# A four-layer graph attention kernel on one core: how the first layer's table is made, and when its first gathers are prepared

## The chip, the core and the metric

The kernel runs on one core of a Trainium2 chip. A core has engines that each work through their own queue of instructions in order: TensorE (PE; its weight loads are listed apart as PEld), VectorE (DVE), ScalarE (ACT), GpSimd (POOL) and SyncE (SP, which here issues most transfers). They meet through semaphores, and share an on-chip memory (SBUF), the matmuls' accumulators (PSUM) and 16 DMA engines.

The metric is device time in microseconds (us) of one execution. Before the change it is 3165.0 us, the median of 9 runs (3157.26 to 3171.3).

## The reference

Four different graph networks are stacked. Each is wrapped in a residual and a layer norm; all use one adjacency matrix `adj` of 4096 x 4096, whose density falls with the index of the row and of the column (0.4% in the mean). There are 256 channels.

```python
def _L0_gnn_ref(x, positions, curv_feats, adj, W, a_l, a_r, Wc, gate):
    N, IN_C, OUT_C, H, CF = (4096, 256, 256, 8, 6)
    h = (x @ W.T).reshape(n, H, D)                      # D = 32
    e_l = jnp.einsum('nhd,hd->nh', h, a_l)
    e_r = jnp.einsum('nhd,hd->nh', h, a_r)
    logits = jax.nn.leaky_relu(e_l[:, None, :] + e_r[None, :, :], negative_slope=0.2)
    curv_pair = jnp.abs(curv_feats[:, None, :] - curv_feats[None, :, :])
    curv_bias = jnp.einsum('ijf,hf->ijh', curv_pair, Wc)
    logits = logits + gate * curv_bias
    logits = jnp.where(mask, logits, jnp.float32(-1000000000.0))
    attn = jax.nn.softmax(logits, axis=1)
    out = jnp.einsum('ijh,jhd->ihd', attn, h)
    return out.reshape(n, H * D)
...
    # --- layer 0 (adj_resnorm) ---
    x = _layernorm(x + _L0_gnn_ref(x, ..., adj, ...), axis=-1)
    # --- layer 1 (adj_resnorm) ---
    x = _layernorm(x + _L1_gnn_ref(x, adj, ...), axis=-1)
    # --- layer 2 (adj_resnorm) ---
    x = _layernorm(x + _L2_gnn_ref(x, adj, ...), axis=-1)
    # --- layer 3 (adj_resnorm) ---
    x = _layernorm(x + _L3_gnn_ref(x, adj, ...), axis=-1)
    return x
```

Layer 1 is attention with one head, layer 2 with four, layer 3 is three attention layers in a row. The change lies in layer 0.

## The kernel before

**Edges in place of a matrix.** Layer 0 uses the sparsity. Rows (the nodes that receive) are cut into 32 row tiles of 128. Row tile 0, the densest, is done as dense matrix work by the generator `rows0` (L448 on; `cj` at L459 are its constants, `g` at L469 its loads, which it shares with later layers through a mask made of `at` tiles). Row tiles 1 to 31 are done edge by edge in `rows_by_edges` (L600 on).

**The projection and the table.** `layer0` (L767 on) first projects the 32 tiles of nodes (the loop over T, after L1139; four tiles share a load `xT`). The result goes to `V0`, 32 tiles of 128 x 278 f32: 8 heads of 33 values (VW = 264), 8 score factors and 6 curvature features. When all tiles are there, the maxima of the scores are taken (`extremes`, whose first step is L1162; `shifts`, `row_factors`), ACT makes exponentials (L1172, L1173), and in one loop over T DVE multiplies each tile by its factors (L1175) and SP writes it to `table0` in DRAM (L1177): 32 transfers of 139 KB, 4.55 MB together. `V0` lies in a pool (`l0_pro`) that ends with the projection.

**The lists.** Which edges a row has is found by class `Lists` (L848 on): a quarter of a row tile of `adj` is loaded (`ai`), ACT turns it to bf16 (L873, L874), DVE searches each piece for its ones (`max_index`, L905), sorts the finds (`max` L920, `match_replace` L922), and small steps end in `from_middle` (L942), which says where each row's edges stand in the row tile's edge list. One list is some 14 to 18 steps of a generator, `edge_lists`. Six steps are taken after every fourth projected tile; the others, while gathers run, by `lane` (14/EDGE_TILES steps per edge tile, so about one list per row tile, which keeps the lead that the projection gave). `prepared(c)`, called when a block asks for its list, takes the steps that are still lacking at once.

**Blocks.** A row tile's edges lie in 9 to 39 edge tiles of 128, cut into 64 blocks of 5 to 9 edge tiles. The steps of a block, in class `Block`:

- `middle`: calls `prepared`, then `u` on ACT (L630), from the constant `number` and `from_middle`
- `spread`: `of_row` on DVE (L635), products to `x` on PE (L639)
- `nodes` (L642 to L654): from `x` and the constants `place` and `count` to the index of every edge, `idx`, on DVE
- `gather` (L659): per edge tile one indirect DMA by POOL, which fetches 128 rows of `table0`; 445 in all. The buffer `g` comes from the pool `l0_got`, which holds three
- `differences`, `pair_terms`, `weights`: the curvature term, with the two tiles `dT` (L619, L620), and the edge's weight
- `values`: `g` times weight on DVE (L689)
- `rows`: `to_row` on ACT (L696, L697)
- `add`: per edge tile a matmul on PE (L702) into the row tile's accumulator `acc`; the last reader of `g`

The loop over the blocks (L735 on) interleaves the steps of blocks i to i+4: `spread` of i+3, then `values` of i, `gather` of i+2, `nodes` of i+3, `add` of i, `middle` of i+4, with `lane` between them. `lane` also issues jobs for later layers, among them single cells of `adj` by indirect DMA on POOL (L1020). `Ends0` finishes row tiles (L320 to L439).

**The order of instructions.** The program's order is not what each engine gets: a scheduler sets the order of the instructions of each engine when the kernel is built, and a new buffer waits for what last used its memory. A pool that is opened where another one ended waits for that pool as a whole.

**The start of `rows_by_edges`.** The constants `number`, `place`, `count` and the two `dT` are made there, after the table's loop: an iota on POOL, casts and memsets on DVE (L614 to L620, L706 to L712). Then the first blocks are prepared:

```python
            for i in range(3):
                at(i, "middle", "spread", "nodes")
                if i < 2:
                    at(i, "gather")
            at(3, "middle")
            at(0, "differences", "pair_terms", "rows", "weights")
```

Of the kernel before, what the change touches and what calls it, by code (L numbers as in the profile page):

```python
# [49 lines left out]
F32 = mybir.dt.float32  # L50
# [3 lines left out]
U16 = mybir.dt.uint16  # L54
I32 = mybir.dt.int32
# [25 lines left out]
def gnn_stack(ctx: ExitStack, tc: tile.TileContext, a: dict, out: bass.AP):  # L81
# [363 lines left out]
                for c, y in zip(cs, ys):  # L445
                    yield from self.proj.steps(c, y)

    def rows0(chunks, ends, ps, ps_s, ps_acc):  # L448

        with ExitStack() as st:
            two = st.enter_context(tc.tile_pool(name="l0_all_two", bufs=2))
            three = st.enter_context(tc.tile_pool(name="l0_all_three", bufs=2))
            got = st.enter_context(tc.tile_pool(name="l0_all_got", bufs=3 * JR))
# [141 lines left out]
            while due:  # L597
                add(*due.pop(0))

    def rows_by_edges(prepared, pair_w, ends, ps, lane, first):  # L600

# [4 lines left out]

        with ExitStack() as st:
            two = st.enter_context(tc.tile_pool(name="l0_two", bufs=2))  # L610
            got = st.enter_context(tc.tile_pool(name="l0_got", bufs=3))
            ps_acc = st.enter_context(tc.tile_pool(name="l0_acc", bufs=2, space=PSUM))
            ps_x = st.enter_context(tc.tile_pool(name="l0_x", bufs=2, space=PSUM))
            number = two.tile([P, BT, P], U16, name="number", bufs=1)  # L614
            place = two.tile([P, max(EDGE_TILES)], F32, name="place", bufs=1)
            count = two.tile([P, P], F32, name="count", bufs=1)
            dTs = [two.tile([ROW1 + 1, P], F32, name=f"dT{k}", bufs=1) for k in range(2)]
            for d in dTs:
                nc.vector.memset(d[0:ROW1], 0.0)  # L619
                nc.vector.memset(d[ROW1:], 1.0)  # L620

            class Block:
                def __init__(self, c, b, t0, n):
# [77 lines left out]
                    for t in range(n):  # L701
                        nc.tensor.matmul(acc, self.to_row[:, t], self.g[:, t, 0:VW], start=self.t0 + t == 0, stop=last and t == n - 1)  # L702

            number_i = two.tile([P, BT * P], I32, name="number_i", tag="to_row")  # L706
            nc.gpsimd.iota(number_i, pattern=[[1, BT * P]], base=0, channel_multiplier=0)
            nc.vector.tensor_copy(number.rearrange("p t r -> p (t r)"), number_i)
            nc.vector.tensor_copy(count, number_i[:, 1:P + 1])
            place_i = two.tile([P, max(EDGE_TILES)], I32, name="place_i", bufs=1)  # L710
            nc.gpsimd.iota(place_i, pattern=[[P, max(EDGE_TILES)]], base=1, channel_multiplier=1)
            nc.vector.tensor_copy(place, place_i)  # L712
# [12 lines left out]
            dense = first(lambda shape, name: ps_x.tile(shape, F32, name=name, tag="x"),  # L725
                          lambda shape, name: ps_acc.tile(shape, F32, name=name, tag="acc0", bufs=1))
            given = 0
            for i in range(3):
                at(i, "middle", "spread", "nodes")
                if i < 2:  # L730
                    at(i, "gather")
            at(3, "middle")
            at(0, "differences", "pair_terms", "rows", "weights")
            late = []
            for i, blk in enumerate(plan):  # L735
                c, n = blk.c, blk.n
                share = n // 4
                ends.put.extend(late)
                late = []
                at(i + 3, "spread")  # L740
                lane(share, c)
                at(i + 1, "differences")
                blk.values()
                at(i + 2, "gather")
                at(i + 1, "pair_terms")
                lane(share, c)
                at(i + 3, "nodes")
                lane(share, c)
                if blk.t0 == 0:
                    ends.until(c - 2)  # L750
# [19 lines left out]
    def layer0(proj):  # L770
        lin = 1.0 - 0.2
        with ExitStack() as st:
# [55 lines left out]
            ones8 = lp.tile([P, 8], BF16, name="ones8")  # L828
            nc.vector.memset(ones8, 1.0)
            near_by = [lp.tile([P, N + 8 * max(sum(k) for k in kinds)], BF16, name="near"), None]  # L830

            adj_pool = st.enter_context(tc.tile_pool(name="l0_adj", bufs=1))
            lists = st.enter_context(tc.tile_pool(name="l0_list", bufs=2))
# [285 lines left out]
            with ExitStack() as pr:  # L1119
# [19 lines left out]
                for T in range(NT):  # L1139
                    if T % ITS == 0:  # L1140
                        xT = xp.tile([P, 2, IC], F32, name="xT")
                        nc.sync.dma_start(xT, a["xT"][:, T * P:T * P + IC].rearrange("(k p) n -> p k n", p=P))
                        nc.vector.tensor_reduce(p0.xs[:, :, T:T + 1], xT, AX.X, ALU.add)
                    drain(p0.product(T, xT[:, :, T % ITS * P:(T % ITS + 1) * P]))
                    if T == ITS - 1:
                        pair_constants(pp, ps_p)
                        nc.vector.memset(by_head[:, :, :, D0:], 1.0)
                        nc.scalar.copy(V[:, :, VW + H0:], curv)
                        none = pp.tile([1, TW], F32, name="none")
                        nc.vector.memset(none, 0.0)  # L1150
                        nc.sync.dma_start(table0[N:N + 1, :], none)
                        drain(proj.prepare(ps))
                    if T % 4 == 3:
                        for _ in range(6):
                            next(edge_lists)
                p0.sums()
                nc.vector.tensor_copy(cs0, p0.cs)
# [2 lines left out]
                with tc.tile_pool(name="l0_st", bufs=1) as sp:  # L1160
                    g = sp.tile([P, NT, H0], F32, name="g0")
                    nc.vector.tensor_sub(g, f2, cw)  # L1162
                    hl, top = extremes(sp, ps_p, f2, H0, more=g)
                    neg_M, v_shift, sc = shifts(sp, top[:, 0, :], top[:, 1, :], lin, "l0")
                    row_factors(sp, ps_p, p0.f1, neg_M, top[:, 1, :], sc, lin, r0_d, side[:, :, 1:1 + H0])
                    nc.vector.tensor_copy(side[:, :, 0:1], neg_row.unsqueeze(1).to_broadcast([P, NC, 1]))
                    nc.vector.tensor_copy(side[:, :, 1 + H0:], curv)
                    nc.vector.tensor_sub(v_shift, v_shift, neg_M)
                    nc.vector.tensor_sub(v_shift, v_shift, top[:, 2, :])
                    v = sp.tile([P, NT, H0], F32, name="v0")  # L1170
                    for h in range(H0):
                        nc.scalar.activation(v[:, :, h], g[:, :, h], AF.Exp, bias=v_shift[:, h:h + 1])  # L1172
                        nc.scalar.activation(V[:, :, VW + h], f2[:, :, h], AF.Exp, bias=sc[:, h:h + 1], scale=-lin)  # L1173
                    for T in range(NT):
                        nc.vector.tensor_tensor(by_head[:, T], by_head[:, T],  # L1175
                                                v[:, T, :].unsqueeze(2).to_broadcast([P, H0, D0 + 1]), ALU.mult)
                        nc.sync.dma_start(table0[T * P:(T + 1) * P, :], V[:, T, :])  # L1177

            at_pool = st.enter_context(tc.tile_pool(name="l0_at", bufs=3))

# [37 lines left out]
            def lane_e(n, c):  # L1218

                for _ in range(n):  # L1220
                    lane(1, (14 / EDGE_TILES[c], 5 / EDGE_TILES[c]))
                    ends.step()

            rows_by_edges(prepared, pair_w, ends, ps, lane_e,
                          lambda ps_s, ps_acc: rows0(FIRST, ends, ps, ps_s, ps_acc))
            proj.sums()
            for k in range(2):
                drain(lanes[k][0])
# [445 lines left out]
    with tc.If(nc.values_load(over[0:1, 0:1], min_val=0, max_val=1) > 0):  # L1674
        with ExitStack() as st:
            pool = st.enter_context(tc.tile_pool(name="all_at", bufs=5))
            for ic in range(-(-DENSE[1] * PW // IC), NIC):
                for load in mask_bytes(pool, ic):
                    load()()
            p1 = first_projection()  # L1680
            ps = tags(st.enter_context(tc.tile_pool(name="all_ps", bufs=1, space=PSUM)), ["pa", "pb"])
            p1.load(st)
            drain(p1.prepare(ps))
            pool = st.enter_context(tc.tile_pool(name="all_acc", bufs=2, space=PSUM))
            ends = Ends0(p1, ps)
            for _ in rows0(NC, ends, ps, lambda shape, name: pool.tile(shape, F32, name=name, tag="s"),
                           lambda shape, name: pool.tile(shape, F32, name=name, tag="acc0")):
                ends.step()
            drain(ends.steps)
            p1.sums()  # L1690
# [54 lines left out]
```

## Time and profile before

| | |
|---|---|
| median of 9 runs | 3165.0 us (3157.26 to 3171.3) |
| the profiled execution: its own time | 3161.5 us |
| its span on the core | 3159.8 us |
| busy PE / PEld | 2574.6 us (81%) / 1800.5 us (57%) |
| busy DVE / ACT / POOL | 2277.9 (72%) / 1329.0 (42%) / 1976.2 us (63%) |
| gathers of layer 0 (L659) | 445, 517.1 us busy, mean 1162 ns |
| cells for later layers (L1020) | 251, 280.2 us busy, mean 1116 ns |
| chain that ended last | PE 51%: L1605 21%, L1515 12%, L1519 8% |

The whole span, split at four points of layer 0 (from the trace; the columns are the stretch, its length, and busy time with count for PE, PEld, DVE, ACT and POOL, then PE's granted clock, the share of time that the DMA engines were busy, and GB/s):

```profile
0.00:105.00 105.00, 58.02 (x328) 47.49 (x328) 78.64 (x403) 40.50 (x129) 6.96 (x107) 0.79 0.53 160
105.00:135.00 30.00, 4.21 (x49) 3.19 (x48) 25.56 (x98) 6.53 (x20) 1.37 (x2) 0.50 0.84 221
135.00:1150.00 1015.00, 636.99 (x5024) 489.21 (x5023) 817.99 (x3088) 585.42 (x1573) 758.20 (x656) 0.74 0.66 198
1150.00:1206.00 56.00, 28.65 (x101) 20.09 (x101) 25.93 (x95) 17.56 (x54) 24.47 (x28) 0.70 0.52 152
1206.00:3160.00 1954.00, 1846.71 (x10568) 1240.55 (x10568) 1329.79 (x3864) 679.00 (x2125) 1185.23 (x1083) 0.97 0.47 134
```

Read it by stage: up to 105 us the projection and the first lists, to 135 the table, to 1150 the gathers, to 1206 the last row tiles, and then layers 1 to 3. The share of busy time of an engine over the whole span is a mean over these stages; only within a stage does it say what limits it. Idle time of an engine is listed with its releaser, the event that came last before the engine went on.

### The profile page before, as it was taken

The page shows a single profiled execution, that of the slowest core. Times are in us where ns is not written, and L with a number is a line of the kernel's source. Part 1 is how long each engine was busy: PE and PEld are TensorE (multiplying, and loading weights), DVE is VectorE, ACT ScalarE, POOL GpSimd, SP SyncE. Part 2 cuts the span into 40 slices and gives each one's busy share as a digit, 9 for nine tenths or more (in the row PEclk, how much of TensorE's full clock was granted, in tenths as well). Part 3 has the DMA queues.
Part 4 walks back from the last instruction along what each step waited for, and adds up shares of the span by engine and source line. Part 5 has one row for each costly group of instructions (what it writes and reads, how often), then busy time and mean ns, then how long its engine had stood idle before and what let it go on. Part 6 is the DMA issues. An engine that isn't in the chain of part 4 may idle for free.

```text
span 3159.8 us, 53737 instructions
## 1 busy us (share of the span) xinstructions
PE 2574.6 (81%) x16067; PEld 1800.5 (57%) x16067; DVE 2277.9 (72%) x7545; ACT 1329.0 (42%) x3895; POOL 1976.2 (63%) x1874
## 2 busy tenths in 40 slices
PE   6266676656666556998999999998899999998997
PEld 5154454444445446996233333333788878887875
DVE  6777877888988856776878788886565556555666
ACT  3365565646666434776212222333222322232334
POOL 0267667777777856772475566651477647755775
PEclk8588776777876677998999999999999999999999
DMA  6567786657676447775333333331554454446654
GB/s 182 163 200 217 234 245 195 208 171 220 198 218 203 115 128 231 200 206 156 105 89 102 95 104 100 100 86 50 172 136 135 114 175 135 135 112 180 166 166 129
DMA packets 345937, 495.65 MB, mean 157 GB/s; under 512 B 120476, under 2 KB 252418, under 8 KB 345634
## 3 DMA queue, kind: packets, MB, share of 16 engines
q0 software_dynamic: 87600, 252.16, 28.6%
q1 hardware_dynamic: 239608, 223.19, 23.5%
q10 hardware_dynamic: 18432, 16.79, 1.6%
q8 instruction: 132, 2.16, 0.3%
q14 instruction: 165, 1.35, 0.1%
HBM read 426.20 MB, written 65.72 MB: 156 GB/s over the span
## 4 chain that ended last, share of the span: by engine, by line
PE 51%; DMA 3%; DVE 2%; ACT 2%; issue 1%; POOL 0%; SPq 0%; ACTq 0%; DVEq 0%; POOLq 0%
PE acc L1605 21%; PE num L1515 12%; PE den L1519 8%; PE ph L209 4%; PE acc L1414 4%; DMA g<-table,pair_idx 3%; PE xT_p L198 1%; PE pr L213 1%; DVE w L1599 1%; PE pt L1537 0%; ACT V L1585 0%; POOL g L1312 0%; DVE y L1617 0%; DVE y L314 0%; DVE bn_st L305 0%
## 5 line engine op out<-in xcount | busy, mean ns | idle before, releaser
L1312 POOL DMA_INDIRECT g<-table,pair_idx x1010 | 1120.4, 1109 | 514.8 <-PE den L1519 103.0
L659 POOL DMA_INDIRECT g<-table,idx x445 | 517.1, 1162 | 195.2 <-issue 119.2
L1605 PE MATMUL acc<-g,w 128*128 128x257 f32 x2448 | 574.1, 382 | 16.6 <-DVE w L1599 15.8
L1605 PEld LDWEIGHTS acc<-g,w 128*128 128x128 f32 x2448 | 458.3, 190 | 93.3 <-DVE w L1599 29.2
L1506 DVE SCALAR_TENSOR_TENSOR w<-R,g,mask 128x256 f32<-128x256 f32 x1004 | 438.9, 488 | 47.8 <-PE den L1519 47.4
L1599 DVE SCALAR_TENSOR_TENSOR w<-R,g,mask 128x256 f32<-128x256 f32 x612 | 292.4, 482 | 238.8 <-PE acc L1605 183.2
L1515 PE MATMUL num<-w,g 128*64 128x256 f32 x2008 | 367.6, 395 | 0.0
L1020 POOL DMA_INDIRECT pair_m<-in_adjT,cell x251 | 280.2, 1116 | 108.0 <-issue 46.6
L702 PE MATMUL acc<-g,to_row 128*128 128x264 f32 x890 | 301.3, 498 | 40.0 <-DVE g L689 31.3
L1605 PE MATMUL acc<-V,w 128*128 128x257 f32 x1152 | 285.2, 388 | 16.9 <-ACT V L1585 9.6
L702 PEld LDWEIGHTS acc<-g,to_row 128*128 128x128 f32 x890 | 214.0, 252 | 93.0 <-DVE g L689 37.8
L1519 PE MATMUL den<-w,g 128*1 128x256 f32 x2008 | 266.5, 378 | 0.0
L1515 PEld LDWEIGHTS num<-w,g 128*64 128x64 f32 x2008 | 140.5, 135 | 196.9 <-DVE w L1506 98.9
L1605 PEld LDWEIGHTS acc<-V,w 128*128 128x128 f32 x1152 | 221.8, 194 | 50.8 <-ACT V L1585 15.9
L1615 ACT ACTIVATE y<-acc,inverse 128x256 f32<-128x256 f32 x96 | 44.7, 466 | 417.5 <-DVE inverse L320 366.8
L209 PE MATMUL ph<-wx,xT 128*128 128x258 f32 (+3 forms) x640 | 184.9, 422 | 36.4 <-ACT xT L200 21.8
L1599 DVE SCALAR_TENSOR_TENSOR w<-R,V,mask 128x256 f32<-128x256 f32 x288 | 137.2, 481 | 90.4 <-PE acc L1605 76.8
L905 DVE FIND_INDEX8 cand<-ones,near 128x8 uint16<-128x520 bf16 (+8 forms) x424 | 195.7, 472 | 0.0
L696 ACT ACTIVATE to_row<-count,side 128x128 f32<-128x128 f32 x445 | 145.4, 391 | 95.7 <-PE acc L702 90.0
L200 ACT ACTIVATE xT<-xT_p 128x128 f32<-128x128 f32 x320 | 86.0, 276 | 198.0 <-PE xT_p L198 188.5
L209 PEld LDWEIGHTS ph<-wx,xT 128*128 128x128 f32 x640 | 125.4, 206 | 67.7 <-ACT xT L200 35.0
L874 ACT ACTIVATE near<-ai 128x64 bf16<-128x64 int32 (+1 forms) x186 | 138.5, 765 | 58.5 <-DMA ai<-in_adj 32.5
(327 smaller groups left out, 4304.9 us busy)
## 6 DMA issues: line engine op xcount, KB each, us to landing
ai<-in_adj SPq DMA_DIRECT2D x124, 512.0 KB
mask<-listed_d SPq DMA_DIRECT2D x228, 128.0 KB
at<-in_adjT SPq DMA_DIRECT2D x96, 256.0 KB
mask<-mask_d SPq DMA_DIRECT2D x128, 128.0 KB
g<-table,pair_idx POOLq DMA_INDIRECT x1010
R<-r_d SPq DMA_DIRECT2D x56, 256.0 KB
table<-V POOLq DMA_DIRECT2D x12, 1032.0 KB
s<-y ACTq DMA_DIRECT2D x96, 128.0 KB
```

The costliest lines, as they stand in the source:

```text
L209: nc.tensor.matmul(ph, xT[:, kt, :], self.wx[:, kt, :], start=kt == 0, stop=kt == 1)
L659: nc.gpsimd.indirect_dma_start(self.g[:, t, :], None, table0[:, :], bass.IndirectOffsetOnAxis(ap=self.idx[:, t:t + 1], axis=0))
L696: nc.scalar.activation(self.to_row[:, t], count, AF.Abs, bias=self.side[:, t, 0:1])
L702: nc.tensor.matmul(acc, self.to_row[:, t], self.g[:, t, 0:VW], start=self.t0 + t == 0, stop=last and t == n - 1)
L905: nc.vector.max_index(cand[:, s], ones8, near[:, at:at + W])
L1020: nc.gpsimd.indirect_dma_start(m[:, :], None, pair_cells, bass.IndirectOffsetOnAxis(ap=cell[:, k:k + 1], axis=0))
L1312: nc.gpsimd.indirect_dma_start(g[:, :], None, self.table[:, :], bass.IndirectOffsetOnAxis(ap=pair_idx[:, at:at + 1], axis=0))
L1506: nc.vector.scalar_tensor_tensor(w[:, h], R[:, h].rearrange("p t i -> p (t i)"), g[:, VW2 + h:VW2 + h + 1], m, ALU.max, ALU.mult)
L1515: nc.tensor.matmul(num[h % 2 * D2:(h % 2 + 1) * D2, h // 2, :], g[:, h * (D2 + 1):h * (D2 + 1) + D2], w[:, h], start=False, stop=last and ...
L1519: nc.tensor.matmul(den[32 * h:32 * h + 1, :], g[:, (h + 1) * (D2 + 1) - 1:(h + 1) * (D2 + 1)], w[:, h], start=False, stop=last)
L1599: nc.vector.scalar_tensor_tensor(w, R[:, q * PW:(q + 1) * PW], g[:, C + 1:C + 2], m, ALU.max, ALU.mult)
L1605: nc.tensor.matmul(t, w[:, it * P:(it + 1) * P], g[:, 0:C + 1], start=k == 0, stop=last)
```

## The change

It has five parts, all in layer 0.

1. `rows0` opens its pools in the stack of its caller and gives back a generator, so that these pools are opened before those of `rows_by_edges`; the PSUM pools reach it later through a dictionary, `banks`.
2. The constants are made at the start of `layer0`, with a temporary pool for the iotas; `count` is called `columns` there.
3. Four list steps, in place of six, follow every fourth projected tile.
4. The table's loop: of every four tiles the last is multiplied by POOL, the others by DVE, and SP writes four tiles in one transfer (8 transfers).
5. `l0_got` holds four buffers. The first three blocks are prepared including `gather`; in the loop `gather` of block i+3 comes right behind its `nodes`, in place of `gather` of i+2 behind `values` of i.

```diff
-    def rows0(chunks, ends, ps, ps_s, ps_acc):
+    def rows0(chunks, ends, ps, ps_s, ps_acc, st):
...
-        with ExitStack() as st:
-            two = st.enter_context(tc.tile_pool(name="l0_all_two", bufs=2))
...
+        two = st.enter_context(tc.tile_pool(name="l0_all_two", bufs=2))
+        three = st.enter_context(tc.tile_pool(name="l0_all_three", bufs=2))
+        got = st.enter_context(tc.tile_pool(name="l0_all_got", bufs=3 * JR))
+        def run():
...
+        return run()
+
-    def rows_by_edges(prepared, pair_w, ends, ps, lane, first):
+    def rows_by_edges(prepared, pair_w, ends, ps, lane, first, banks, consts):
...
-            got = st.enter_context(tc.tile_pool(name="l0_got", bufs=3))
+            got = st.enter_context(tc.tile_pool(name="l0_got", bufs=4))
...
-            number = two.tile([P, BT, P], U16, name="number", bufs=1)
-            place = two.tile([P, max(EDGE_TILES)], F32, name="place", bufs=1)
-            count = two.tile([P, P], F32, name="count", bufs=1)
-            dTs = [two.tile([ROW1 + 1, P], F32, name=f"dT{k}", bufs=1) for k in range(2)]
-            for d in dTs:
-                nc.vector.memset(d[0:ROW1], 0.0)
-                nc.vector.memset(d[ROW1:], 1.0)
+            number, place, count, dTs = consts
...
-            number_i = two.tile([P, BT * P], I32, name="number_i", tag="to_row")
-            nc.gpsimd.iota(number_i, pattern=[[1, BT * P]], base=0, channel_multiplier=0)
...
             for i in range(3):
-                at(i, "middle", "spread", "nodes")
-                if i < 2:
-                    at(i, "gather")
+                at(i, "middle", "spread", "nodes", "gather")
...
                 blk.values()
-                at(i + 2, "gather")
                 at(i + 1, "pair_terms")
                 lane(share, c)
-                at(i + 3, "nodes")
+                at(i + 3, "nodes", "gather")
...
+            number = lp.tile([P, BT, P], U16, name="number")
+            place = lp.tile([P, max(EDGE_TILES)], F32, name="place")
+            columns = lp.tile([P, P], F32, name="columns")
+            with tc.tile_pool(name="l0_iota", bufs=1) as ip:
+                number_i = ip.tile([P, BT * P], I32, name="number_i")
+                nc.gpsimd.iota(number_i, pattern=[[1, BT * P]], base=0, channel_multiplier=0)
...
+            dTs = [lp.tile([ROW1 + 1, P], F32, name=f"dT{k}") for k in range(2)]
+            for d in dTs:
+                nc.vector.memset(d[0:ROW1], 0.0)
+                nc.vector.memset(d[ROW1:], 1.0)
...
                     if T % 4 == 3:
-                        for _ in range(6):
+                        for _ in range(4):
                             next(edge_lists)
...
                     for T in range(NT):
-                        nc.vector.tensor_tensor(by_head[:, T], by_head[:, T],
-                                                v[:, T, :].unsqueeze(2).to_broadcast([P, H0, D0 + 1]), ALU.mult)
-                        nc.sync.dma_start(table0[T * P:(T + 1) * P, :], V[:, T, :])
+                        (nc.gpsimd if T % 4 == 3 else nc.vector).tensor_tensor(
+                            by_head[:, T], by_head[:, T], v[:, T, :].unsqueeze(2).to_broadcast([P, H0, D0 + 1]), ALU.mult)
+                        if T % 4 == 3:
+                            nc.sync.dma_start(table0[(T - 3) * P:(T + 1) * P, :].rearrange("(t p) c -> p t c", p=P), V[:, T - 3:T + 1, :])
...
-            rows_by_edges(prepared, pair_w, ends, ps, lane_e,
-                          lambda ps_s, ps_acc: rows0(FIRST, ends, ps, ps_s, ps_acc))
+            banks = {}
+            dense = rows0(FIRST, ends, ps, lambda shape, name: banks["x"].tile(shape, F32, name=name, tag="x"),
+                          lambda shape, name: banks["acc"].tile(shape, F32, name=name, tag="acc0", bufs=1), st)
+            rows_by_edges(prepared, pair_w, ends, ps, lane_e, dense, banks, (number, place, columns, dTs))
```

More of the change, by code (lines that the diff above doesn't have):

```diff
@@ L446, in all @@
                     yield from self.proj.steps(c, y)
-    def rows0(chunks, ends, ps, ps_s, ps_acc):
-        with ExitStack() as st:
-            two = st.enter_context(tc.tile_pool(name="l0_all_two", bufs=2))
-            three = st.enter_context(tc.tile_pool(name="l0_all_three", bufs=2))
-            got = st.enter_context(tc.tile_pool(name="l0_all_got", bufs=3 * JR))
+    def rows0(chunks, ends, ps, ps_s, ps_acc, st):
[3 more added lines that the diff above has]
+        def run():
             cjs = []
@@ L702, in add @@
                         nc.tensor.matmul(acc, self.to_row[:, t], self.g[:, t, 0:VW], start=self.t0 + t == 0, stop=last and t == n - 1)
-            number_i = two.tile([P, BT * P], I32, name="number_i", tag="to_row")
[L707 to L712, printed above, removed]
             plan = [Block(c, b, t0, n) for c in range(FIRST, NC) for b, (t0, n) in enumerate(blocks_of(c))]
@@ L723, in at @@
                         getattr(plan[i], w)()
-            dense = first(lambda shape, name: ps_x.tile(shape, F32, name=name, tag="x"),
-                          lambda shape, name: ps_acc.tile(shape, F32, name=name, tag="acc0", bufs=1))
+            banks.update(acc=ps_acc, x=ps_x)
+            dense = first
             given = 0
             for i in range(3):
-                at(i, "middle", "spread", "nodes")
-                if i < 2:
-                    at(i, "gather")
+                at(i, "middle", "spread", "nodes", "gather")
             at(3, "middle")
@@ L830, in layer0 @@
             near_by = [lp.tile([P, N + 8 * max(sum(k) for k in kinds)], BF16, name="near"), None]
+            number = lp.tile([P, BT, P], U16, name="number")
[4 more added lines that the diff above has]
+                nc.gpsimd.iota(number_i, pattern=[[1, BT * P]], base=0, channel_multiplier=0)
+                nc.vector.tensor_copy(number.rearrange("p t r -> p (t r)"), number_i)
+                nc.vector.tensor_copy(columns, number_i[:, 1:P + 1])
+                place_i = ip.tile([P, max(EDGE_TILES)], I32, name="place_i")
+                nc.gpsimd.iota(place_i, pattern=[[P, max(EDGE_TILES)]], base=1, channel_multiplier=1)
+                nc.vector.tensor_copy(place, place_i)
+            dTs = [lp.tile([ROW1 + 1, P], F32, name=f"dT{k}") for k in range(2)]
+            for d in dTs:
+                nc.vector.memset(d[0:ROW1], 0.0)
+                nc.vector.memset(d[ROW1:], 1.0)
             adj_pool = st.enter_context(tc.tile_pool(name="l0_adj", bufs=1))
@@ L1686, in gnn_stack @@
             for _ in rows0(NC, ends, ps, lambda shape, name: pool.tile(shape, F32, name=name, tag="s"),
-                           lambda shape, name: pool.tile(shape, F32, name=name, tag="acc0")):
+                           lambda shape, name: pool.tile(shape, F32, name=name, tag="acc0"), st):
                 ends.step()
```

## The prediction

> **What bounds the kernel now.** I read the profiled execution (span 3159.8 us, device time 3161.5 us) in this order: the slices and the chain on the page, windows over layer 0, the order in time around the table, the waits of POOL. The chain ends with 51% of the span on PE, all of it after 1263 us, where layers 1 to 3 run. It says nothing of layer 0, whose end is their start, so layer 0 is read by windows. Their columns are the stretch, its length, and busy time with count for PE, PEld, DVE, ACT and POOL, then PE's granted clock, DMA share and GB/s:
>
> ```profile
> 60.00:78.00 18.00, 16.82 (x96) 13.44 (x95) 15.71 (x77) 10.93 (x38) 0.00 (x0) 0.91 0.68 227
> 78.00:90.00 12.00, 0.16 (x1) 0.00 (x0) 12.00 (x70) 4.69 (x10) 0.00 (x0) 0.60 0.38 124
> 105.00:116.00 11.00, 0.52 (x1) 0.00 (x0) 11.00 (x34) 0.40 (x3) 0.00 (x0) 0.50 0.90 272
> 200.00:240.00 40.00, 27.80 (x243) 22.70 (x242) 30.37 (x81) 25.04 (x68) 31.40 (x24) 0.83 0.75 224
> 600.00:640.00 40.00, 24.04 (x186) 18.79 (x187) 34.64 (x127) 23.00 (x61) 31.78 (x28) 0.79 0.71 220
> ```
>
> Before the gathers DVE sets the pace: the projection is over at 78 us, and DVE has 12 us of list work left before the score maxima that need the projection. From 105 us the table is a transfer at 272 GB/s. In the gather stage POOL sets the pace: 28 gathers of 128 rows in 40 us, each with about 0.3 us before it, are 31.78 + 28 x 0.3 = 40.2 us, the whole window. These are the points in time, and three places where POOL stands:
>
> ```profile
> 104.80 7.30 DVE L1175 TENSOR_TENSOR V<-V,v 128x264 f32<-128x264 f32 x21
> 126.26 0.17 DVE L619 MEMSET dT<- 64x128 f32 x1 [2.71 <-DMA g<-table]
> 126.69 1.19 POOL L707 IOTA number_i<- 128x1280 int32 x1 [118.42 <-DMA g<-table]
> 127.91 0.83 DVE L708 CAST number<-number_i 128x1280 uint16<-128x1280 int32 x1
> 128.77 0.83 ACT L630 ACTIVATE u<-number,from_middle 128x640 f32<-128x640 uint16 x1 [9.10 <-DMA at<-in_adjT]
> 135.28 1.03 POOL L659 DMA_INDIRECT g<-table,idx  x1 [7.23 <-DVE hit L648]
> 379.36 0.94 POOL L659 DMA_INDIRECT g<-table,idx  x1 [8.92 <-PE acc L702]
> 401.76 0.94 POOL L659 DMA_INDIRECT g<-table,idx  x1 [13.10 <-DVE rhs L983]
> 1149.56 0.95 POOL L659 DMA_INDIRECT g<-table,idx  x1 [0.30 <-issue]
> 1205.97 5.54 PE L1414 MATMUL acc<-Vp,w 128*128 128x258 f32 x28 [3.49 <-ACT Vp L1380]
> ```
>
> The table is scaled from 104.8, has landed by 126.3 (DVE's wait ends there; the name in the bracket is the last event, not the whole wait), the first gather goes out at 135.3, the last at 1149.6, and layer 1 multiplies at 1206. From 135.28 to 1150.51 POOL issues 656 indirect transfers (445 gathers, 211 cell loads for later layers) in 1015 us. Adding up all idle pieces over 0.45 us, less 0.3 us each, gives 57 us in which POOL stood still; the other 958 us are its work. The waits of POOL (total us, times, longest) name the largest part:
>
> ```profile
> POOL g L659 <- issue: 114.0, 360, 3.4
> POOL g L659 <- PE acc L702: 25.1, 12, 8.9
> POOL g L659 <- DVE rhs L983: 13.1, 1, 13.1
> POOL g L659 <- DVE there L926: 7.3, 2, 7.0
> ```
>
> A wait on PE acc is a wait for a gather buffer: the matmuls at L702 are its last readers.
>
> **The change, part by part.** *Four list steps in place of six* with each fourth projection tile: 16 fewer steps, about one list. I compared the order of the built programs on DVE up to the first scaling of the table. The changed one has there 16 fewer searches (L905: three of row tile 3's at 0.41, 0.61 and 0.61 us from one start to the next, thirteen of tile 4's at 0.18 to 0.41, together 6.1 us), 6 fewer maxima and 5 fewer replacements (0.57 us a pair, 3.1 us), and some 25 small ones (2.9 us): 12.1 us. DVE is busy 58 of the 61 us from 44 to 105, so all of it comes off, if the projection does not hold it back. The latter is close: from its end at 78.3 to 104.8 the row maxima, exponentials and their waits take 104.8 - 90.5 = 14.3 us (L1162, the first to need the projection, starts at 90.54), so the table can't start before 92.6. 104.8 - 12.1 = 92.7. I take 12 us, with ends 6 (the projection late) and 13. The list isn't gone: DVE does it in the gather stage, where it is busy 30 to 35 of 40 us.
>
> *Constants early.* Iota (0.43 us wait and 1.19), cast (0.83) and four memsets stood between the landed table and the first u at 128.77: 2.5 us, now done in DVE's idle time before 40 us (busy 17 of 40 there; that idle time is the cover, without it they cost the 2.5 us again).
>
> *First blocks beside the table.* In the built program the first u (L630, now L627), the first load of at, and DVE's memsets of cj each still wait for all eight table transfers: the new buffers lie in the memory of the pool that holds V, and they wait for the pool as a whole. So nothing is prepared beside the table. In DVE's queue two conversions of at now stand ahead of the first index (0.42 us each); the second at landed at 131.27 in the old trace, 4.5 us after its issue. Landed table to first gather took 9.0 us; I get 8 (gain 1; ends: loss 2, from these waits, and gain 2.5, from the constants). If the blocks really were ahead, about 8 us more would go.
>
> *Table in 8 transfers, every fourth tile scaled by POOL.* DVE scales 24 tiles at 0.354 us (32 in 11.3 us): 8.5 us. POOL's nearest row is L1527, 128x256 in f32, 862 ns: 8 take 7.1 us, side by side. The transfers are 4.55 MB in 21.3 us from first scaling to landing; they and not the scaling are the limit, and R's 0.5 MB now comes after them (2 us at 272 GB/s), while the first transfer now waits for four tiles (1.3 us). SP issues 8 in place of 32, which were hidden. I take 0; ends: gain 4, loss 8. The loss is POOL held back until DVE is done (8.5 us). That POOL can be held is in the trace:
>
> ```profile
> 146.64 0.95 POOL L659 DMA_INDIRECT g<-table,idx  x1 [0.30 <-issue]
> 147.25 1.52 DVE L689 TENSOR_TENSOR g<-g,w 128x1320 f32<-128x1320 f32 x1
> 147.89 1.70 POOL L659 DMA_INDIRECT g<-table,idx  x1 [0.30 <-issue]
> ```
>
> A gather of 0.95 us takes 1.70 beside a long two-operand product on DVE. The Trainium skill, SBUF — State Buffer, section "Who interferes with whom", speaks against this edit: a VectorE operation with two SBUF inputs and a GpSimd operation that reads SBUF exclude each other for a whole instruction. By that rule the two shares add up, 8.5 + 7.1 = 15.6 us; taking turns, one group of four would be ready every 1.95 us, still under the 2.3 us that its transfer takes.
>
> *Four gather buffers, gather right behind the indices.* The buffer that the gather of block i+3 needs is that of block i-1, as for block i+2 before: its release is the same, but POOL runs one block (5 to 9 gathers of 1.25 to 1.4 us, 7 to 12 us) further ahead. Isolated waits shorter than that should go: 4.3 at 165, 3.9 at 184, 3.1 near 260, 4.4 at 767, 2.4 at 921 and 2.7 near the end, together 21 us. In the cluster from 370 to 453 (34 us) one block's lead, 9 us, is saved once. That is 30. The lists take some back: in the old program no list is ever late when a block asks for it, in the new one the lists of row tiles 3, 4, 5 and 8 are finished on demand, two or three steps each, and ACT, which is in order, then holds everything behind u. The trace has one such case, tile 9, in the middle of that cluster:
>
> ```profile
> 476.72 0.20 DVE L942 TENSOR_SCALAR from_middle<-mid 128x1 f32<-128x1 f32 x2
> 476.89 1.15 ACT L630 ACTIVATE u<-number,from_middle 128x1024 f32<-128x1024 uint16 x1
> ```
>
> The u before it began at 459.22, 17.7 us earlier, against 13 to 16 us for its neighbours: 2 to 5 us late. Behind u on ACT stand to_row, dT and e of earlier blocks, and for these PE's products wait, which free the buffers. Six rows at 3 us are 18. Fourth buffer less late lists: gain 12, ends 35 and a loss of 25.
>
> *What is the same*: 211 cell loads stand before the last gather in both programs; from the last gather to layer 1 (1150.5 to 1206) it is one chain through L666 to L1375; layers 1 to 3 are untouched and move as a whole.
>
> Sum: 12 + 1 + 0 + 12 = 25 us, 3161.5 - 25 = 3136.5 for an execution like the profiled one. The median of the nine runs is 3.5 us above it: 3140.
>
> **Rivals.** (1) Only the start moves: the buffer's gain and the late lists cancel. For it: POOL already fills whole windows. Against it: 57 us of idle. 13 us: 3152. (2) Slower, by late lists: with one list less of a lead, u waits in each of row tiles 3 to 9, and what is behind u on ACT waits along. For it: the lead shrinks in the old trace from 44 us (tile 4: ready at 233.4, used at 277.3) to 28 (tile 6) and 0 (tile 9), and a list is worth 35 us there. Against it: three filled buffers cover 20 to 30 us. At 8 us a row, seven rows cost 56; the start gives 13 and the buffer, in its isolated part, 21: 22 us slower, 3187. It decides above (13 + 21) / 7 = 4.9 us a row. (3) The buffer works in full and lists are never late: 13 + 30 to 35 us, 3120. (4) POOL's eighth of the table starves behind DVE: 8 us back, 3148; inside the range.
>
> **How the numbers follow.** Chances: forecast 0.45, (3) 0.13, (4) 0.07, (1) 0.14, no net change since the lists take it all 0.09, slower 0.12. Within 0.2%, 6.3 us, is what a measurement here can't tell from no change. Faster is the first four less the part of (1) that loses the start too, 0.78; same 0.10, slower 0.12. Range: the low end takes all good ends, 13 + 2.5 + 4 + 35 = 54.5, to 3110, of which I cut 2 for their chance together; the high end reaches into no change, 3165. Outside are most of (2) and little else.
>
> **What would show it.** First scaling at 92 to 94 us, landed table at 113 to 116, first gather at 121 to 125, last at 1120 to 1128, layer 1 at 1176 to 1186. Waits of POOL for PE acc below 10 us, no second idle of 13 us. If POOL's idle pieces still sum to 57, the buffer was worth nothing; if u is seen to wait for from_middle in tiles 3 to 9 and POOL's idle grows, (2) is right; if the first gather comes after 130, the start was mis-sized. A change after layer 1's start of more than 5 us would mean that something outside layer 0 moved.

## The result, and the profile after

The changed kernel is slower: 3200.1 us median (3185.3 to 3206.9, 10 runs) against 3166.5 us (31 runs of before); the ratio of the means is 1.0095, 95% interval 1.0082 to 1.0109. The forecast was 3140 us, with a range to 3165; the time lies outside it, on the other side of before.

Five points in time split the two profiled executions (the first four are starts):

| us | before | after | moved by |
|---|---|---|---|
| first scaling on DVE | 104.80 | 89.25 | -15.6 |
| first gather | 135.28 | 115.56 | -19.7 |
| last gather | 1149.56 | 1187.45 | +37.9 |
| layer 1's first matmul | 1205.97 | 1248.11 | +42.1 |
| span | 3159.8 | 3197.5 | +37.7 |

The start gained 19.7 us. From the first to the last gather it took 1071.9 us in place of 1014.3: 57.6 us lost. The way from there to layer 1 took 4.2 us more, layers 1 to 3 took 4.4 us less.

Where the 57.6 us were lost shows when that time is split at the first gather of block 19 (row tile 5, blocks counted from 0) and that of block 25 (row tile 7). By the latter POOL has loaded 25 cells in both kernels. The last columns are POOL's idle time before gathers, beyond the usual 0.3 us:

| stretch | before, us | after, us | lost | idle before | idle after |
|---|---|---|---|---|---|
| first gather to block 19 | 226.5 | 241.5 | 15.0 | 11 | 38 |
| block 19 to block 25 | 94.2 | 107.0 | 12.8 | 34 | 43 |
| block 25 to the last gather | 693.6 | 723.4 | 29.8 | 8 | 29 |

The changed kernel in order of time, with the points shown of before:

```profile
88.75 6.05 POOL L1178 TENSOR_TENSOR V<-V,v 128x264 f32<-128x264 f32 x8 [78.16 <-ACT v L1175]
89.25 0.42 DVE L1178 TENSOR_TENSOR V<-V,v 128x264 f32<-128x264 f32 x1
...
108.24 0.83 ACT L627 ACTIVATE u<-number,from_middle 128x640 f32<-128x640 uint16 x1 [5.88 <-DMA table<-V]
...
115.56 1.04 POOL L656 DMA_INDIRECT g<-table,idx  x1 [20.76 <-DMA at<-in_adjT]
...
1248.11 5.36 PE L1420 MATMUL acc<-Vp,w 128*128 128x258 f32 x28 [3.04 <-ACT Vp L1386]
```

The first `u` still waits for the table's transfers (its bracket), as read from the built program. The same windows as before, and one of 20 us that has no counterpart there (stretch, length, busy time with count of PE, PEld, DVE, ACT, POOL, PE's clock, DMA share, GB/s):

```profile
200.00:240.00 40.00, 26.64 (x149) 19.87 (x150) 24.13 (x81) 22.22 (x63) 30.53 (x26) 0.71 0.76 226
400.00:420.00 20.00, 0.61 (x1) 0.11 (x1) 4.02 (x14) 0.00 (x0) 9.39 (x10) 0.50 0.83 238
600.00:640.00 40.00, 28.32 (x209) 21.01 (x207) 34.56 (x147) 25.37 (x70) 31.77 (x28) 0.79 0.76 231
```

At 600 us POOL fills its window as before. Between 400 and 420 PE and ACT do nothing, and POOL ends its last gathers, while the DMA engines are 83% busy. The timeline of that stretch names the reason (SPq is SP's queue of transfers):

```profile
400.51 0.38 SPq L847 DMA_DIRECT2D ai<-in_adj  x1
...
404.99 0.43 SPq L397 DMA_DIRECT2D at<-in_adjT  x1
...
407.84 0.43 DVE L402 TENSOR_SCALAR mb<-at 128x512 uint8<-128x512 int32 x1 [3.72 <-DMA at<-in_adjT]
408.30 0.80 SPq L404 DMA_DIRECT2D mask_d<-mb  x2
...
416.95 0.43 SPq L469 DMA_DIRECT2D g<-table  x1
...
420.57 0.45 PE L481 MATMUL cj_p<-ident,c 128*96 128x128 f32 x1 [19.55 <-DVE c L480]
...
450.19 0.94 POOL L656 DMA_INDIRECT g<-table,idx  x1 [38.05 <-PE acc L699]
```

SP works in order. Its mask jobs for later layers are a load of `at`, a conversion on DVE, and two stores; the store waits for the conversion, the conversion for the load. Six of them, 2.7 us each, stand between the list load at 400.51 and row tile 0's load of `g` at 416.95. PE's next instruction needs that `g` (over `c`, L480, at 420.31), so PE stands 20 us, with every list, index and `add` behind it. POOL has no gather to issue for 38 us: when PE goes on, the list of row tile 7 (430.79), its `u` (430.96) and the index (449.29) still have to follow. In the kernel before the same instruction of PE waits 4.5 us at most.

POOL's longest waits name another thing wrongly. The waits of POOL from 100 to 1260 us (total us, times, longest):

```profile
POOL g L656 <- PE acc L699: 47.0, 5, 38.1
...
POOL g L656 <- PE e_p L672: 10.1, 1, 10.1
```

Read as in the prediction, the first would be a wait for a buffer. But set each gather that begins a block beside DVE's cast of its index:

```profile
154.15 0.16 DVE L651 CAST idx<-node 128x5 int32<-128x5 f32 x1
155.06 1.11 POOL L656 DMA_INDIRECT g<-table,idx  x1 [10.09 <-PE e_p L672]
...
449.29 0.15 DVE L651 CAST idx<-node 128x8 int32<-128x8 f32 x1
```

The gather after the 10 us wait comes 0.75 us after its index, that after the 38 us wait (450.19) 0.75 us after its index. I did this for all waits over 1.5 us at the first gather of a block. In the changed kernel there are 17, together 110 us, and all 17 end 0.7 to 0.8 us after the index. In the kernel before there are 9, 48 us: four (14 us) end so. The other five (34 us) have had their index for longer, and each ends 0.3 us behind the last matmul at L702 that reads the buffer. So it is with the gather at 379.36, a line of the prediction; these are its index and the last readers of its buffer:

```profile
373.19 5.89 PE L702 MATMUL acc<-g,to_row 128*128 128x264 f32 x16 [5.41 <-DVE g L689]
377.95 0.15 DVE L654 CAST idx<-node 128x7 int32<-128x7 f32 x1
```

In the changed kernel all 17 gathers have had their buffer free for 11 to 34 us.

### The profile page after: what moved, and what is told of

Its sections match the earlier page's. It is cut to its first block, busy times and chain, and to the rows that moved or that the text cites. A ratio compares the mean times of both kernels' runs of the same rounds, so it can differ in the third digit from the quotient of the medians.

```text
span 3197.5 us, 53723 instructions
## 1 busy us (share of the span) xinstructions
PE 2603.0 (81%) x16067; PEld 1811.0 (57%) x16067; DVE 2277.8 (71%) x7537; ACT 1327.8 (42%) x3895; POOL 1977.0 (62%) x1882
## 4 chain that ended last, share of the span: by engine, by line
PE 51%; DMA 3%; DVE 2%; ACT 2%; issue 1%; POOL 0%; SPq 0%; ACTq 0%; DVEq 0%; POOLq 0%
PE acc L1611 21%; PE num L1521 12%; PE den L1525 8%; PE ph L209 4%; PE acc L1420 4%; DMA g<-table,pair_idx 3%; PE xT_p L198 1%; PE pr L213 1%; DVE w L1605 1%; PE pt L1543 0%; ACT V L1591 0%; DVE y L1623 0%; POOL g L1318 0%; DVE y L314 0%; DVE bn_st L305 0%
## 5 line engine op out<-in xcount | busy, mean ns | idle before, releaser
L699 PE MATMUL acc<-g,to_row 128*128 128x264 f32 x890 | 315.0, 516 | 33.7 <-DVE g L686 25.9
L699 PEld LDWEIGHTS acc<-g,to_row 128*128 128x128 f32 x890 | 223.6, 263 | 94.0 <-DVE g L686 31.5
L693 ACT ACTIVATE to_row<-columns,side 128x128 f32<-128x128 f32 x445 | 146.7, 392 | 118.2 <-PE acc L699 114.4
```

The lines of the kernel that those rows point to most:

```text
L693: nc.scalar.activation(self.to_row[:, t], count, AF.Abs, bias=self.side[:, t, 0:1])
```

## The experiments

They ran later, on four chips (numbered in the table), and the kernel before took 3650 to 3700 us in all of them, at a granted clock of 0.82 to 0.84 in place of 0.88. There e3, which is before but for the fourth buffer, gathers from 137.6 to 1342.7 us and has 2237 us left from layer 1 on; before had 1954 in the first runs. So each kernel is compared with before on its own chip and in its own group of runs, and for the first runs the shares are inferred.

In the table, L481 is PE's longest wait there, in us, among those that end within 0.2 us of the copy that makes `c`, whatever name the profile gives them; "gathers" and "cells" are POOL's idle time (beyond the usual 0.3 us) before gathers and before cell loads, from the first to the last gather of the profiled execution. The ratios come from all runs, these three columns from one execution each.

| run (chip) | buffers, steps, other | ratio to before, 95% | L481 | gathers | cells |
|---|---|---|---|---|---|
| before (first runs) | 3, 6 | 1 | 4.5 | 53 | 4 |
| after (first runs) | 4, 4 | 1.0095 (1.0082-1.0109) | 19.6 | 110 | 5 |
| c1 (7) | after again | 1.0047 (1.0008-1.0087) | 17.6 | 227 | 114 |
| e1 (0) | 4, 6 | 0.9989 (0.9955-1.0023) | 7.1 | 152 | 111 |
| e1b (7) | 4, 6 | 0.9965 (0.9932-0.9998) | 7.3 | 174 | 111 |
| f1 (3) | 4, 6 | 0.9962 (0.9934-0.9990) | 7.0 | 160 | 116 |
| e2 (0) | 3, 4 | 0.9972 (0.9946-0.9999) | 15.5 | 215 | 50 |
| e2b (7) | 3, 4 | 0.9961 (0.9927-0.9995) | 15.4 | 234 | 80 |
| f2 (3) | 3, 4 | 0.9964 (0.9933-0.9995) | 15.5 | 227 | 83 |
| e3 (0) | before, 4 buffers | 0.9979 (0.9947-1.0010) | 4.2 | 179 | 97 |
| e4 (0) | before, 4 steps | 0.9968 (0.9938-0.9999) | 14.9 | 215 | 52 |
| e4b (7) | before, 4 steps | 0.9995 (0.9967-1.0023) | 15.4 | 232 | 83 |
| e5 (8) | 4, 4, thin masks | 0.9923 (0.9890-0.9957) | 1.6 | 166 | 118 |
| f3 (3) | 4, 4, thin masks | 0.9968 (0.9937-0.9999) | 0.4 | 195 | 121 |
| e6 (8) | before, thin masks | 0.9934 (0.9905-0.9963) | 4.9 | 185 | 64 |
| e7 (8) | 4, 4, row 0's loads on ACT | 0.9974 (0.9947-1.0001) | 1.1 | 172 | 120 |
| e8 (8) | 4, 6, thin masks | 0.9971 (0.9942-1.0000) | 15.4 | 147 | 105 |
| f4 (3) | 3, 4, thin masks | 0.9873 (0.9824-0.9923) | 2.3 | 185 | 56 |
| g1 (0) | 3, 4, thin masks | 0.9849 (0.9814-0.9885) | 1.6 | 190 | 77 |
| g2 (0) | 3, 4, thin, row 0 on ACT | 0.9874 (0.9838-0.9909) | 4.3 | 171 | 78 |

**Steps and buffers apart: e1 to e4.** Theory A was that missing list steps make the lists late; theory B that the order behind the fourth buffer stalls.

```diff
# e1: after, with
-                        for _ in range(4):
+                        for _ in range(6):
# e2: after, with
-            got = ... name="l0_got", bufs=4    at(i + 3, "nodes", "gather")
+            got = ... name="l0_got", bufs=3    at(i + 2, "gather") behind values, at(i + 3, "nodes")
# e3: before, with the reverse of e2; e4: before, with the reverse of e1
```

> The changed kernel with six list steps again behind every fourth projected tile, everything else as changed. Theory A (the lists are late: from row tile 2 to 10 each first u starts 0.2 to 1 us after its from_middle, and the stage is paced by them): the first gather comes about 12 us later than the changed kernel's 115.6, and the lists have their lead back, tile 8's is ready before 450 (474.4 in the changed kernel, 430.2 before); 3140 to 3165 us. Theory B (the order behind the fourth buffer, with the gather behind the indices, is what stalls, as in the 38 us without a gather from 412 to 450 while one load for row tile 0 stands behind mask stores in SP's queue): the stall stays and the time is 3200 to 3215.

> The changed kernel with three gather buffers and the gather at its old place, still with four list steps, early constants and the new table loop. Theory A: lists as late as in the changed kernel, 3185 to 3210 us. Theory B: the order of before behind a start that is 20 us earlier, 3140 to 3155.

> The kernel before with four gather buffers and the gather right behind the indices, nothing else. Theory A: POOL's isolated waits for a buffer go, the lists keep most of their lead, 3140 to 3165 us. Theory B: 3185 to 3205.

> The kernel before with four list steps in place of six, nothing else. Theory A: the first gather comes 12 us earlier (near 123), the lists of row tiles 3 to 9 are late, 3175 to 3205 us. Theory B: 12 us are kept, 3150 to 3158.

All four times lie within 0.4% of before, which confirms neither theory as written. The traces tell more. The stall comes with the four steps and not with the buffer: e2 and e4, with three buffers, have it (PE waits 15 us); e1 and e3, with four, have not (7 and 4 us). So B is wrong about it. e4 has its first gather 17.7 us before that of e3 beside it (119.9 against 137.6), and its last one 11.2 us before: it gives back a part of its start.

**The same with the changed kernel beside them: c1, e1b, e2b, e4b.**

> The changed kernel once more, as the control for the three beside it: the first four experiments ran on a chip where the kernel before took 3650 us, 15% more, and no variant differed from it by 0.4%. Both theories: 1.0095 of before on a chip like the first one; on a slow chip no expectation.

> The changed kernel with six list steps. Theory A (late lists pace row tiles 2 to 10): 30 to 60 us less than the changed kernel beside it, 0.992 to 1.0 of before. Theory B (the order behind the fourth buffer stalls): 0 to 15 us more than the changed kernel.

> The changed kernel with three gather buffers and the gather at its old place. Theory A: within 15 us of the changed kernel. Theory B: 45 to 60 us less than the changed kernel, 0.995 of before.

> The kernel before with four list steps alone. Theory A: the lists of row tiles 2 to 9 are late and take more than the 12 us that the start gives, 1.003 to 1.013 of before. Theory B: the 12 us are kept, 0.996 of before.

Six steps take 31 us off the changed kernel (3717.0 to 3686.2), as A expects; three buffers take 26 us off it, more than A allows and less than B. e4b is 1.0 of before, below A's range and above B's. The profiled execution of e2b is the slowest of its runs (3712.6 us), so the trace of e2b doesn't show what its 26 us come from. In e2b, with three buffers, the stall of the changed kernel is there in the same order, first on SP, then DVE, PE and POOL:

```profile
457.89 0.43 SPq L469 DMA_DIRECT2D g<-table  x1
460.93 0.20 DVE L480 COPY c<-g 128x96 f32<-128x96 f32 x1
461.19 0.45 PE L481 MATMUL cj_p<-ident,c 128*96 128x128 f32 x1 [15.44 <-DVE c L480]
...
474.79 0.94 POOL L656 DMA_INDIRECT g<-table,idx  x1 [31.18 <-DVE inverse L320]
```

**Taking the stall away without touching steps or buffers: e5 to e8.** Theory C is the reading of the trace above: mask jobs in SP's queue ahead of the loads. "Thin" leaves all 96 mask jobs in, but spreads them over three times as many edge tiles.

```diff
# e5, e6 (before), e8 (with six steps): thin masks
                     job(jobs, begun, 7)
-                    job(dense_jobs, dense_begun, 1)
+                    if beat[0] % 3 == 0:
+                        job(dense_jobs, dense_begun, 1)
# e7: row tile 0's loads on another queue
-                        nc.sync.dma_start(g, table0[k * P:(k + 1) * P, :])
+                        nc.scalar.dma_start(g, table0[k * P:(k + 1) * P, :])
(and m likewise)
```

> The changed kernel with the mask jobs of later layers (load at, conversion on DVE, two stores) one at every third edge tile in place of one at every tile; the same 96 jobs. Theory C (until 436 us SP goes through the mask jobs in step with DVE, 2.3 to 3 us each, and the loads for the lists and for row tile 0 stand behind them; with two list steps fewer this stops PE at L481 and everything behind it): the wait of PE for row tile 0's load (L481) falls below 6 us, POOL's wait of 30 to 38 us near row tile 7 goes, 0.985 to 0.997 of before. Theory A (the missing list steps themselves, as work on DVE and ACT, are what is late): 1.000 to 1.0095 of before.

> The kernel before with the mask jobs one at every third edge tile. Theory C: the cluster of POOL's waits from 370 to 453 us shrinks, 0.990 to 0.997 of before. Theory A: 0.997 to 1.003.

> The changed kernel with the two loads of row tile 0's dense work (g and m) issued from ACT's queue in place of SP's. Theory C: PE's wait at L481 falls from 20 to below 6 us, and POOL's wait near row tile 7 from 38 (31 to 33 in the runs with four steps) to below 20; 0.995 to 1.002 of before. Theory A: the list of row tile 7 is as late as it was, 1.003 to 1.0095 of before.

> The changed kernel with six list steps and the mask jobs one at every third edge tile. Theory C: 0.980 to 0.994 of before. Theory A: as with six steps alone, 0.992 to 1.000 of before.

PE's waits at L481 (total us, times, longest) in c1, and in f3 with thin masks:

```profile
PE cj_p L481 <- DVE c L480: 18.2, 2, 17.6
```

```profile
PE cj_p L481 <- DVE c L480: 0.4, 1, 0.4
```

e7 changes two lines and no list step: the wait falls to 1.1 us, POOL's longest wait for a block to 14 us, and the time lies as C expects, as it does in e5. So neither the missing list work nor the buffer makes PE's stall; the place of one load in SP's queue does. The changed kernel itself didn't run on this chip, so how much time e5 and e7 take off it isn't shown; c1, on another chip, had 1.0047. e6 shows that the masks cost the kernel before something too. e8 missed: its time lies in A's range, and it has a 15.4 us wait at L481 again, at 521 us, so thinning moves the loads without a guarantee.

**The fourth buffer: f1 to f4, g1, g2.**

> The changed kernel with six list steps, again. Stall at row tile 0's load as the cause of the loss: no wait of PE above 8 us at L481; on a chip with 3166 us before 0.992 to 1.000, on a slow one 0.995 to 1.000. Fourth buffer as the cause: 1.003 to 1.010.

> The changed kernel with three buffers and the old place of the gather, again. Stall as the cause: PE waits 15 to 20 us at L481 and POOL some 30 us behind it, on a chip with 3166 us before 1.003 to 1.010. Fourth buffer as the cause: 0.990 to 0.998.

> The changed kernel with the mask jobs at every third edge tile, again. Stall as the cause: no wait above 6 us at L481, 0.985 to 0.997 of before on either kind of chip. Fourth buffer as the cause: 1.000 to 1.008.

> The changed kernel with three buffers, the old place of the gather and thinned mask jobs. If the fourth buffer is worth something once the stall is gone, 5 to 25 us more than the run with thinned masks beside it; if the fourth buffer costs, 5 to 25 us less; within 5 us it does nothing.

> The changed kernel with three buffers, the old place of the gather and thinned mask jobs, again. If the fourth buffer is a loss of its own: 0.984 to 0.991 of before, as in f4. If f4 was a matter of its few runs: 0.992 to 0.998, as thinned masks with four buffers.

> As g1, with row tile 0's two loads issued from ACT's queue too. If thinning has already taken the stall away: within 0.4% of g1. If row tile 0's loads still stop PE there: 0.4 to 1% less than g1.

f1 and f3 lie where the stall as the cause has them, f2 where the buffer has: it has the stall (PE waits 15.5 us and POOL 31 us behind it, as expected), and with three buffers that doesn't make it slower than before. On one chip, f4 takes 41 us less than f3 (3650.8, in 4 runs, against 3691.9), more than the 5 to 25 us that I expected: once the masks are thin, the fourth buffer with the early gather is a loss. g1 repeats f4's ratio on another chip. With six steps the buffer does nothing that can be told (e3: 0.9979, interval over 1).

Where the loss lies is in the table's last columns. Before gathers, POOL's waits are not clearly shorter with four buffers than with three (c1 227 and e2b 234; f3 195 and f4 185); they only end otherwise. Of the waits over 1.5 us at the first gather of a block, 28 of 28 in c1, 34 of 34 in f3 and 23 of 25 in e3 end within 0.8 us of the index; with three buffers it is 11 of 34 in f2 and 16 of 38 in f4. Before cell loads, which stand behind the gathers in POOL's queue, POOL stands 97 to 121 us in all nine later runs with four buffers, and 50 to 83 in all nine with three. Most of these waits are for the cells' own buffers, of which there are nine (`pair_m`): in f3, 19 of 22 over 1.5 us end 0.3 us behind DVE's conversion of the cell nine before (L1027), in f4 all 12.

g2 is within 0.4% of g1: with three buffers and thin masks nothing of the stall is left.

g1 is the best version: 1.5% under before on its chip. Whether it is so where before takes 3166 us was not seen.

## Why the prediction was wrong

**The start** was right in kind, and too small: 19.7 us for 13. Of it 15.6 lie before the scaling, where I had 12.1 and held the projection's end at 78.3 us for a floor. It was none: the list steps on DVE had slowed the projection too. It now ended at 71.9, and the first maximum that needs it came at 75.72, in place of 90.54. The table took 19.0 us from scaling to landing for 21.5, the way to the first gather 7.3 for 9.0.

**POOL's eighth of the table** (of 32 tiles) didn't starve. POOL was done in 6.05 us; DVE's 24 tiles took 11.3 us where I counted 8.5. Up to 95 us, while POOL worked, the two took turns: a product of each every 0.78 us, those of DVE 0.85 us long, where DVE alone starts one every 0.34 us. So the two did hold each other up, as the Trainium skill, SBUF — State Buffer, section "Who interferes with whom", has it for such a pair; both were done after 11.8 us, where I made 15.6 of its rule, and what POOL takes alone no run here shows. The whole stayed under the 19 us that the transfers take. Rival 4 falls.

**The fourth buffer** is the step that failed: "its release is the same, but POOL runs one block further ahead", 30 us. POOL can't run ahead of its index. In the new order the gather of block i+3 stands behind `nodes` of i+3, whose index DVE makes after `differences` of i+1 and `values` of i, which wait for gathers that have just landed. In the old order an index was an iteration old when its gather came. The index of block 4, made at 154.15, shows it; ahead of it in DVE's queue stands a wait for the gathers of block 3:

```profile
147.72 0.20 DVE L663 TENSOR_TENSOR d<-g,side 128x36 f32<-128x36 f32 x1 [5.49 <-DMA g<-table,idx]
```

So the waits for a buffer are gone, all 34 us of them, and waits for the index have taken their place: 110 us, where there were 14. e3 prices the term, on chip 0: the fourth buffer with the early gather, and nothing else, takes 0.2% off the kernel before (interval from 0.5% off to 0.1% on), where 30 us would be 0.8%.

The waits of before were misread as well: "A wait on PE acc is a wait for a gather buffer". Of the five over 1.5 us before a block that the profile puts down to PE's `acc`, two end with the buffer (8.9 and 2.1 us) and three with the index (4.6, 4.2 and 3.2); the other three waits for a buffer have other names, `rhs` with its 13.1 us among them. Of the isolated waits that I added up to 21 us, those of 4.3 and 3.9 us at 165 and 184 end with the index, and that of 2.4 us at 921 stands before a cell. The name in a wait was the last event near it.

**The lists** I counted at 18 us, as `u` on ACT held by a late list. From row tile 3 to 10 `u` does start 0.2 to 1 us behind its list, as rival 2 has it. In every run with four steps it starts within 7 us, and mostly within 1 us, behind its list there; f4 and g1, the two fastest by their ratio, are among them. So late lists alone are not the loss. What was not in the sum at all is the stall: with other list steps in the order, row tile 0's load stands behind six mask jobs in SP's queue, which stops PE for 20 us and POOL for 38. It takes both. e8 has the early lists of six steps (5 to 15 us of lead at row tiles 8 and 9) and a wait of PE of 15.4 us at 521, but from 500 to 545 us POOL waits 4.8 us at most; the kernels with late lists and a stall have a wait of POOL of 30 to 38 us.

The stall isn't all of the loss. It lies in the second stretch of the table in the section on the result, where 12.8 of the 57.6 us were lost, since before has its waits for a buffer there; 45 us were lost in the other two, where POOL's idle time grew by 48 us, by waits for the index. In the later runs six steps in place of four take 43 us off the time from the first to the last gather (e1b against c1), of which 18 lie in that stretch, and thin masks 44 us (f4 against f2), of which 33 do. Which part of the change took how much in the first runs, no run isolates.

**Rival 2**, at 0.12, gave 3187 and was nearest: it had the side and the late lists, but not the load in SP's queue through which they cost, nor the index. That layers 1 to 3 move as a whole was right (4.4 us).

What stays open: why the cells' buffers come free later with four gather buffers (in the first runs POOL waited 4 us for cells before, and 5 after), why six steps with four buffers lose nothing, and the shares in the first runs.

## What to carry to other kernels

Before a buffer is added, set the start of each waiting instruction beside the end of each thing that it needs, and ask which of them comes last once the buffer is there. Here the buffers were free 11 to 34 us ahead, and every wait ended with the index. Moving a prefetch to right behind the producer of its index gives away the lead that the index had. And in an in-order queue of transfers, jobs that go in step with another engine (load, convert, store) hold up every load behind them; a list of steps taken out elsewhere is enough to move a critical load behind them.

## What the runs showed of the hardware

The kernel before took 3166 us in the first runs and 3650 to 3700 in all later ones; on chip 0 it took 3650.6 us in one group of runs and 3697.7 in another. The work was the same as far as the profiles tell (DVE busy 2278 us in before's own and 2270 in e4's, which differs by the list steps; POOL 1976 and 1966), with more idle time. The change cost 0.95% in the first runs and 0.47% on chip 7 (interval 0.08 to 0.87%). Why they differ stays open. A load of 256 KB queued in a stretch where the DMA engines were 83% busy kept DVE waiting 3.7 us, while PE and ACT stood still. DVE and POOL, each multiplying tiles of 128x264 with two operands in SBUF, took turns at one of each every 0.78 us.
